# Edge counts with a row of degrees, and an own division of PSUM for the heads of the first attention

## The chip, the cores and the metric

The kernel runs on one core of a Trainium2 chip. The core has five engines with a program each: TensorE (PE in the profile; PEld is its weight load), VectorE (DVE), ScalarE (ACT), GpSimd (POOL) and SyncE (SP, which here issues DMAs). Each engine works through its instructions in their order and waits on semaphores for the others. The metric is the device time of one execution in microseconds (us): 1857.35 us is the median of three runs of the kernel before (1856.94 to 1857.70).

## The reference

The reference is a stack of four blocks on a graph of 625 nodes with 768 features and a list of edges (src, dst); each block is a graph layer and then an expert or feed-forward layer, each behind a layer norm and added to x. The change lies in the first graph layer alone, an attention of 12 heads with 64 features per head:

```
hv = h.reshape(n, H, DIN)                          # h = layernorm(x), H = 12
ft = einsum('nhd,od->nho', hv, W)
a1 = sum(ft * attn_l, -1);  a2 = sum(ft * attn_r, -1)
e = leaky_relu(a1[src] + a2[dst], 0.2)
m = segment_max(e, dst)
w = exp(e - m[dst])
alpha = w / maximum(segment_sum(w, dst)[dst], 1e-16)
agg = segment_sum(alpha[:, :, None] * ft[src], dst)
out = relu((agg + einsum('nhd,od->nho', hv, W_res)).reshape(n, H * DOUT))
x = x + out
```

Later layers (two graph convolutions among them) need the in-degree of each node: deg = segment_sum(1, dst), with a loop edge added, and its reciprocal root.

## The kernel before

All of it is one program, whose functions below issue instructions; a scheduler then decides the order in which they stand on each engine, and places the semaphores. Lines are those of the kernel before. Nodes are held as 5 tiles (t or s) of P = 125.

**Edge counts (L863 to L894).** The graph is turned into a dense matrix A[src, dst] of edge counts (AT, in f32, 125 x 5 x 625). The edges come as 85 chunks of 125. For each chunk DVE makes a one-hot matrix of the sources (ohs, L868, four rotating buffers) and one of the destinations (ohd, L863, where one column stands for two destinations: the second counts 4096), and PE multiplies them tile by tile (L875, five matmuls a chunk, 32 chunks accumulated in PSUM). Then ACT copies the sums out as integers (L883), DVE takes them apart (L885, L886) and adds them to AT (L892, L894). Between chunks PE also projects the features (L802, L810, L833).

**Before the heads.** ACT and DVE take the logarithm of the counts (L630, L631), and PE turns AT tile by tile for a mask (`mask_tile`, 25 transposes, L639), which ACT changes to 0 or a large number (L642).

**One head** is these steps, and the loop at L993 to L1026 issues them staggered over heads:

- `score` (L654 on ACT, L658 on POOL): weights of all pairs, from a row of a2 loaded by DMA and the logarithms.
- `gat_largest`: PE spreads a1 as a row over the partitions (L156, five transposes into a PSUM buffer, `spread_with`); DVE takes the largest over the neighbours (L666, one instruction per tile) and makes from it the offset u (L672, L673).
- `gat_exp`: PE spreads u as a row (L156 again, operand gat_u), DVE subtracts it (L686; one instruction for heads 0 to 9, five for heads 10 and 11), ACT takes the exponential (L688, five instructions).
- `gather`: PE multiplies the weights with the features (L138, ten matmuls of two passes each), ACT copies the result out (L943, gat_o).
- `back`: PE turns it (L958), DVE takes the reciprocal of the sum (L961) and adds each tile to res (L963). Every second head ACT clips the pair (L974) and POOL adds it to x (L1019); for the last pairs DVE does so (L1013, L982). DVE takes statistics of x for the next layer norm (L978).

**Degrees (L922 to L931).** For each tile of destinations five matmuls (L927) of AT with a column of ones, so 25 in all; ACT copies the five columns out (L931). They are called in the loop at i == 2.

**After the heads (L1026 to L1035).** POOL converts AT for later layers and adds the loops (L1028 to L1031), SP stores it (L1032), ACT and DVE make the reciprocal root of the degrees (L1033 to L1035). The last head's `back` also normalises x tile by tile and turns it for the next layer (L194 to L206, then L213 on PE and L217 on ACT). The next layer's first matmuls are L145.

**PSUM.** Every step above that writes PSUM takes its buffer from `ps()`: four rotating buffers of 128 x 1024 f32, two banks each, so the whole of PSUM. A step waits until the last reader of the buffer's user four turns before is done.

Of the kernel before, what the change touches and what calls it, by code (L numbers as in the profile page):

```python
# [19 lines left out]
N = 625  # L20
P = 125
# [18 lines left out]
class Net:  # L40
# [6 lines left out]
    def __init__(self, ctx, tc, a, out):  # L47
        self.tc, self.nc, self.a, self.out = tc, tc.nc, a, out
        self.turn = 0
        self.ctx = ctx  # L50
        nc = self.nc
        self.const = ctx.enter_context(tc.tile_pool(name="const", bufs=1))
        self.small = ctx.enter_context(tc.tile_pool(name="small", bufs=2))
        self.rows = ctx.enter_context(tc.tile_pool(name="rows", bufs=2))
        self.xnp = ctx.enter_context(tc.tile_pool(name="xnp", bufs=2))
        self.psum = ctx.enter_context(
            tc.tile_pool(name="psum", bufs=4, space=bass.MemoryType.PSUM)
        )
# [36 lines left out]
        self.iD = self.dram.tile([1, 2], U32, name="iD")  # L95
        self.counts = ExitStack()
        pool = self.counts.enter_context(tc.tile_pool(name="atr", bufs=1))
        self.ATr = pool.tile([128, NT, N + 1], F32R, name="ATr")
        self.which = pool.tile([2, 1], U32, name="which")
        self.many = pool.tile([P, NT], F32, name="many")  # L100
        self.open_counts()

    def open_counts(self):
        self.exact = ExitStack()
        self.AT = self.exact.enter_context(self.tc.tile_pool(name="at", bufs=1)).tile(
            [P, NT, N], F32, name="AT"
        )

    def ps(self):
        return self.psum.tile([128, 1024], F32, tag="ps", name="ps")  # L110

    @staticmethod
    def nv(t, rows, cols=P):
# [34 lines left out]

        return self.spread_with(col, rows)[0]

    def spread_with(self, col, rows):

        p = self.ps()
        pv = self.nv(p, rows)
        for t in range(NT):
            self.nc.tensor.transpose(  # L156
                pv[:, t, :], col(t).to_broadcast([P, rows]), self.ident[:P, :P]
            )
        return pv, p[:rows, NT * 128 : NT * 129]

    def row(self, name, cols, src=None):

# [467 lines left out]
        nc.scalar.activation(r, self.AT[:, s, :], AF.Ln, bias=self.tiny[:P], scale=2.0)  # L630
        nc.vector.scalar_tensor_tensor(r, r, BIG, r, ALU.mult, ALU.min)  # L631

    def mask_tile(self, mb, t, act=False):


        nc = self.nc
        pv = self.nv(self.ps(), P)
        for s in range(NT):
            nc.tensor.transpose(pv[:, s, :], self.AT[:, s, TILES[t]], self.ident[:P, :P])  # L639
        m = self.n3(mb[:, t, :])  # L640
        if act:
            nc.scalar.activation(m, pv, AF.Relu, bias=self.large[:P], scale=-BIG)  # L642
        else:
            nc.vector.tensor_scalar(m, pv, 0.5, BIG / 2, ALU.is_lt, ALU.mult)

    def gat_scores(self, w, a1, a2row, lc, a8=None):

# [12 lines left out]
    def gat_largest(self, pool, mb, a1, a2, row=None):  # L660

        nc = self.nc
        row, m = row or self.spread_with(lambda t: a1[:, t : t + 1], P)
        for t in range(NT):
            junk = pool.tile([P, N], F32, tag="junk", name="junk", bufs=1)
            nc.vector.tensor_tensor_reduce(  # L666
# [9 lines left out]
    def gat_exp(self, w, a1, u, a2=None, pieces=1):  # L676

        nc = self.nc
        if a2 is None:
            a2 = self.small.tile([P, NT], F32, tag="gat_2", name="gat_2")  # L680
            nc.scalar.activation(a2, a1, AF.Copy, scale=0.2)
        row = self.spread(lambda t: u[:, t : t + 1], P)
        w4 = w.rearrange("p t (k c) -> p t k c", c=P)
        for s in range(0, NT, NT // pieces):
            ws = w4[:, s : s + NT // pieces]
# [5 lines left out]
    def L0_gnn(self):  # L691
# [5 lines left out]
        with ExitStack() as ctx:  # L697
# [13 lines left out]
            with ExitStack() as c1:  # L711
# [141 lines left out]

                AT = self.AT
                G = 32
                for c0 in range(0, NC, G):
                    cs = range(c0, min(c0 + G, NC))
                    acc = [halves(self.ps()[:P])[:, :, 0:HN] for _ in range(3)]  # L860
                    for c in cs:
                        ohd = op.tile([P, HN + 1], BF16, tag="ohd", name="ohd")
                        nc.vector.tensor_scalar(  # L863
                            ohd, iota[:, 0 : HN + 1], key[:, c : c + 1], wt[:, c : c + 1],
                            ALU.is_equal, ALU.mult,
                        )
                        ohs = op.tile([P, NW], BF16, tag="ohs", name="ohs")
                        nc.vector.tensor_scalar(  # L868
                            ohs, iota, ef[:, 0, c : c + 1], None, ALU.is_equal
                        )  # L870
                        oh[0] = ohd
                        for piece in pieces.get(c, ()):
                            piece()
                        for j in range(NT):
                            nc.tensor.matmul(  # L875
                                acc[j // 2][:, j % 2, :], ohs[:, TILES[j]], ohd[:, 0:HN],
                                start=c == cs[0], stop=c == cs[-1],
                            )
                    first = c0 == 0
                    for j in range(3):  # L880
                        n = 2 if j < 2 else 1
                        raw = cp.tile([P, 2, HN], I32, tag="raw", name="raw", bufs=3)[:, 0:n]
                        nc.scalar.copy(raw, acc[j][:, 0:n])  # L883
                        hi = cp.tile([P, 2, HN], I32, tag="hi", name="hi")[:, 0:n]
                        nc.vector.tensor_scalar(hi, raw, 12, None, ALU.arith_shift_right)  # L885
                        nc.vector.tensor_scalar(raw, raw, 4095, None, ALU.bitwise_and)  # L886
                        at = AT[:, 2 * j : 2 * j + n]
# [9 lines left out]
            for s in range(NT):  # L897
                self.log_counts(lc, s)

            row = self.spread_with(lambda t: al[:, t, 0, 0:1], P)  # L900
            for t in range(NT):
                self.mask_tile(mb, t, act=True)
            self.prepare(router="L0_ffn_router")

            guard = big.tile([DH + 1, 1], F32, name="guard")
# [15 lines left out]

            def degrees():  # L922

                p = self.ps()[:P, 0:NT]
                for t in range(NT):
                    for s in range(NT):
                        nc.tensor.matmul(  # L927
                            p[:, t : t + 1], self.AT[:, s, TILES[t]], self.ones[:P, 0:1],
                            start=s == 0, stop=s == NT - 1,
                        )  # L930
                nc.scalar.copy(self.deg, p)  # L931

            def gather(h):

                w = ws[h]
                pv = self.nv(self.ps(), DH + 1)
                self.mm_nodes(
                    pv, [ft[:, s, h, :] for s in range(NT)],
                    [self.n3(w[:, s, :]) for s in range(NT)],
# [7 lines left out]
            def back(h, then=None):  # L947

                o = outs[h]
                p = self.ps()[:P, 0 : NT * 128].rearrange("p (t c) -> p t c", c=128)  # L950
                rden = self.small.tile([P, NT, 1], F32, tag="rden", name="rden")
                hs = slice(h * DH, (h + 1) * DH)
                for part in (range(4), range(4, NT)) if then else (range(NT),):
# [36 lines left out]
            for i in range(H + 4):  # L990
# [4 lines left out]
                if 0 <= i - 2 < H:  # L995
# [1 line left out]
                    self.gat_exp(  # L997
                        ws[h], a1[h], us[h], a1s[:, 0, :, h], pieces=1 if i < H else NT
                    )
                if i == 2:  # L1000
                    degrees()
                steps = [(back, i - 4), (gather, i - 3)]
                for f, h in steps if i < H else reversed(steps):
# [4 lines left out]
                if i == H + 1:  # L1008

                    for g in range(H // 2 - 1):  # L1010
# [11 lines left out]
                        for t in range(NT):  # L1022
                            stats(t, g)
            back(H - 1, then=last)

            for t in range(NT):  # L1026
                at, r = AT[:, t, :], self.ATr[:P, t, 0:N]
# [1575 lines left out]
```

## Time and profile before

| What | Value |
|---|---|
| median of three runs | 1857.35 us (1856.94 to 1857.70) |
| the profiled execution | 1859.18 us |
| its span, first to last instruction | 1857.5 us |
| mean granted clock of TensorE | 0.986 |
| busy share of the span, PE / DVE / POOL / ACT | 96% / 61% / 36% / 29% |
| chain that ended last: matmuls of L145 | 64% of the span |
| first counting matmul L875 in the chain | 24.89 us |
| start of the first L686 | 111.87 us |
| start of head 9's L686 | 196.67 us |
| first L145 of the next layer | 233.01 us |

The span is shorter than the execution's time by what lies around it (1.68 us). A line of the time line has the start, the duration, the engine, the line of the code, the operation, output and inputs with their shapes, and a count; in brackets stands how long the engine was idle before it and what ended that. PE's granted clock is a share of its full speed: 1.00 or, in some stretches, 0.50.

### The profile page before, as it was taken

What the parts mean: (1) busy time and instruction counts of PE and PEld (TensorE: products, weight loads), DVE (VectorE), ACT (ScalarE), POOL (GpSimd) and SP (SyncE); (2) the same over time, 40 slices, a digit from 0 to 9 for tenths busy, and PEclk for the clock granted to TensorE, in tenths of its full rate; (3) what the DMA queues carried; (4) which work ended last, traced back from release to release, by engine and by line L of the source; (5) the groups of instructions that cost most, each with busy time, mean ns of one, the idle gap of its engine ahead of it and who ended that gap; (6) DMA issues with size and microseconds to landing.
All of it is one profiled execution on the core that took longest, in us unless ns stands there. A gap on an engine that the chain in (4) does not pass through costs nothing.

```text
span 1857.5 us, 21937 instructions
## 1 busy us (share of the span) xinstructions
PE 1783.6 (96%) x8274; PEld 1275.4 (69%) x8274; DVE 1138.7 (61%) x2307; ACT 543.0 (29%) x979; POOL 667.1 (36%) x532
## 2 busy tenths in 40 slices
PE   8978899999999999999999999999999999999998
PEld 7854466557677766655776787878768888556765
DVE  8789866657666765575486655564756555154452
ACT  2468831114244433111211131231314323111200
POOL 0068666435410035753225322221335222401550
PEclk9969999999999999999999999999999999999999
DMA  2040143120300014514142211011012111020311
GB/s 55 24 146 35 57 116 115 55 85 23 97 26 27 1 53 144 159 41 136 42 136 94 85 43 60 26 60 35 6 40 68 54 56 39 0 102 26 110 59 33
DMA packets 71696, 119.29 MB, mean 64 GB/s; under 512 B 8609, under 2 KB 38531, under 8 KB 71591
## 3 DMA queue, kind: packets, MB, share of 16 engines
q1 hardware_dynamic: 71266, 117.80, 19.7%
q8 instruction: 65, 1.06, 0.2%
q14 instruction: 41, 0.33, 0.1%
q10 hardware_dynamic: 260, 0.09, 0.0%
q0 software_dynamic: 64, 0.01, 0.0%
HBM read 114.30 MB, written 3.58 MB: 63 GB/s over the span
## 4 chain that ended last, share of the span: by engine, by line
PE 80%; DVE 11%; ACT 4%; DMA 2%; issue 2%; POOL 0%; SPq 0%; DVEq 0%; ACTq 0%
PE ps L145 64%; PE ps L2081 2%; PE ps L1707 2%; PE ps L1739 2%; DVE av_junk L1541 2%; PE ps L875 2%; PE ps L138 2%; PE ps L1726 2%; DVE gat_w L686 1%; ACT gat_w L688 1%; PE ps L213 1%; PE ps L156 1%; DMA x<-in_x 1%; DMA av_w<-in_L_gnn_W 1%; PE ps L810 1%
## 5 line engine op out<-in xcount | busy, mean ns | idle before, releaser
L428 POOL TENSOR_TENSOR S<-w 128x384 f32<-128x384 f32 x40 | 41.9, 1052 | 390.8 <-PE ps L145 290.5
L145 PE MATMUL ps<-w,xT 128*125 128x384 f32 (+3 forms) x440 | 141.2, 474 | 0.0
L145 PE MATMUL ps<-xT,w 128*128 128x313 f32 x480 | 139.1, 430 | 0.7 <-ACT pr L1715 0.7
L145 PE MATMUL ps<-T,w 128*128 128x313 f32 x408 | 122.4, 430 | 8.9 <-DVE U L448 7.7
L658 POOL TENSOR_TENSOR gat_w<-gat_w,xT 125x625 f32<-125x625 f32 x60 | 86.2, 1472 | 118.4 <-DVE xT L631 96.3
L145 PEld LDWEIGHTS ps<-w,xT 128*125 128x125 f32 (+1 forms) x440 | 81.8, 188 | 52.5 <-issue 11.3
L145 PEld LDWEIGHTS ps<-xT,w 128*128 128x128 f32 x480 | 90.1, 191 | 33.9 <-ACT pr L1715 0.9
L145 PE MATMUL ps<-T,S 128*128 128x313 f32 x348 | 103.7, 431 | 1.7 <-DVE T L408 1.4
L145 PEld LDWEIGHTS ps<-T,w 128*128 128x128 f32 x408 | 75.4, 189 | 41.5 <-DVE U L448 10.1
L145 PE MATMUL ps<-xT,S 128*128 128x313 f32 x336 | 101.1, 430 | 0.0
L145 PE MATMUL ps<-w,S 128*125 128x384 f32 (+1 forms) x292 | 99.2, 486 | 0.0
L145 PE MATMUL ps<-w,hg 128*125 128x384 f32 x288 | 96.3, 486 | 0.0
L145 PE MATMUL ps<-hh,gat_w 125*125 125x257 f32 (+1 forms) x400 | 89.7, 379 | 0.0
L145 PE MATMUL ps<-w,x2T 128*125 128x384 f32 (+1 forms) x280 | 84.3, 450 | 0.9 <-DVE gat_u L673 0.9
L1541 DVE CUSTOM_DVE_ANT_0 av_junk<-av_w,av_a 128x512 bf16<-128x512 f32 (+1 forms) x80 | 81.5, 1018 | 3.7 <-DMA av_w<-in_L_gnn_W 1.8
L145 PEld LDWEIGHTS ps<-T,S 128*128 128x128 f32 x348 | 63.9, 189 | 28.7 <-ACT lt L456 4.4
L145 PEld LDWEIGHTS ps<-w,S 128*125 128x125 f32 (+1 forms) x292 | 54.8, 188 | 39.0 <-issue 0.7
L145 PEld LDWEIGHTS ps<-hh,gat_w 125*125 125x125 f32 x400 | 73.4, 187 | 11.0
L145 PEld LDWEIGHTS ps<-xT,S 128*128 128x128 f32 x336 | 62.0, 189 | 24.3 <-DVE lt L448 2.2
L145 PEld LDWEIGHTS ps<-w,hg 128*125 128x125 f32 x288 | 53.6, 188 | 36.5 <-issue 0.6
L138 PE MATMUL ps<-gat_w,ft 125*65 125x500 f32 (+1 forms) x240 | 69.8, 447 | 5.2 <-DVE gat_w L686 3.5
L875 PE MATMUL ps<-ohd,ohs 125*125 125x313 bf16 x425 | 64.0, 304 | 8.8 <-DVE ohs L868 8.8
(485 smaller groups left out, 3800.0 us busy)
## 6 DMA issues: line engine op xcount, KB each, us to landing
w<-in_L_ffn_phiT SPq DMA_DIRECT2D x8, 1536.0 KB
w<-in_L_gnn_W SPq DMA_DIRECT2D x8, 1536.0 KB
gate<-gD SPq DMA_DIRECT2D x24, 312.5 KB
w<-in_L_ffn_w SPq DMA_DIRECT2D x6, 1152.0 KB
w<-in_L_gnn_W SPq DMA_DIRECT2D x6, 1152.0 KB
av_w<-in_L_gnn_W SPq DMA_DIRECT2D x24, 256.0 KB
av_w<-in_L_gnn_W SPq DMA_DIRECT2D x16, 384.0 KB
w<-in_L_ffn_w SPq DMA_DIRECT2D x3, 1536.0 KB
```

The lines of the kernel that those rows point to most:

```text
L138: self.nc.tensor.matmul(pv[:, s, :], lhs[i], rhs[i][:, s, :], start=i == 0, stop=i == n - 1)
L145: self.nc.tensor.matmul(out, lhs[i], rhs[i], start=i == 0, stop=i == n - 1)
L156: self.nc.tensor.transpose(pv[:, t, :], col(t).to_broadcast([P, rows]), self.ident[:P, :P])
L213: nc.tensor.transpose(pv[:, k, :P], src[:, k * 128 : (k + 1) * 128], self.ident[:P, :P])
L428: nc.gpsimd.tensor_tensor(S1, A21, A22, ALU.add)
L658: nc.gpsimd.tensor_tensor(w[:, s, :], w[:, s, :], lc[:, s, :], ALU.add)
L875: nc.tensor.matmul(acc[j // 2][:, j % 2, :], ohs[:, TILES[j]], ohd[:, 0:HN], start=c == cs[0], stop=c == cs[-1],)
L1541: nc.vector.tensor_tensor_reduce(junk, wt, row, 1.0, 0.0, ALU.mult, ALU.add, dst)
L1707: nc.tensor.matmul(sv[r][:, s, :], qk[half[r], 0, TILES[t]], self.n3(qk[half[r], 1, :])[:, s, :], start=True, stop=True,)
L1726: nc.tensor.transpose(tv[:, s, :], pr[:, s * P : (s + 1) * P], self.ident[:P, :P])
L1739: nc.tensor.matmul(ov[half[r]], v[:, s, h * DH : (h + 1) * DH], pT[r][:, s, :], start=s == 0, stop=s == NT - 1,)
L2081: nc.tensor.matmul(pv[:, j, :], zTs[t][:, k, :], w2[k // 3][:, k % 3, js], start=k == 0, stop=False,)
```

## The change

The counting keeps four fixed one-hot buffers for the sources, two columns wider, and the extra columns are set to one once. The last of a chunk's five matmuls has 127 rows out in place of 125, so that row 126 of AT's last tile holds the number of edges of each destination. The degrees are then five matmuls (one per tile of destinations) that pick that row with a column of the identity matrix, and are called at i == 3. PSUM has a new division after the counting: one fixed buffer "gathered", one fixed buffer "turned", and two rotating ones; `gather` takes the first, `back` and the degrees the second, all rows the rotating ones. After the last `back` has been issued the division goes back to four rotating buffers. The masks' transposes are issued by source tile for three destination tiles at a time.

```
+    def open_psum(self, kept=()):
+        self.banks.close()
+        self.psum = self.banks.enter_context(
+            self.tc.tile_pool(name="psum", bufs=1, space=bass.MemoryType.PSUM)
+        )
+        self.kept = {k: self.psum.tile([128, 1024], F32, tag=k, name="ps") for k in kept}
+
+    def ps(self, kept=None):
+        if kept in self.kept:
+            return self.kept[kept]
+        return self.psum.tile(
+            [128, 1024], F32, tag="ps", name="ps", bufs=4 - len(self.kept)
+        )
...
-    def mask_tile(self, mb, t, act=False):
+    def mask_tile(self, mb, *ts, act=False):
...
-        pv = self.nv(self.ps(), P)
+        pvs = {t: self.nv(self.ps(("gathered", "turned", None)[t % 3]), P) for t in ts}
         for s in range(NT):
-            nc.tensor.transpose(pv[:, s, :], self.AT[:, s, TILES[t]], self.ident[:P, :P])
...
+            for t in ts:
+                nc.tensor.transpose(
+                    pvs[t][:, s, :], self.AT[:, s, TILES[t]], self.ident[:P, :P]
+                )
...
-        row = self.spread(lambda t: u[:, t : t + 1], P)
+        row = self.spread_with(lambda t: u[:, t : t + 1], P, "offsets")[0]
...
+                senders = [ep.tile([P, NW + 2], BF16, name=f"ohs{i}") for i in range(4)]
+                for ohs in senders:
+                    nc.gpsimd.memset(ohs[:, NW:], 1.0)
...
                         for j in range(NT):
+                            R = P if j < NT - 1 else P + 2
                             nc.tensor.matmul(
-                                acc[j // 2][:, j % 2, :], ohs[:, TILES[j]], ohd[:, 0:HN],
-                                start=c == cs[0], stop=c == cs[-1],
+                                acc[j // 2][:R, j % 2, :], ohs[:, j * P : j * P + R],
+                                ohd[:, 0:HN], start=c == cs[0], stop=c == cs[-1],
                             )
...
+            self.open_psum(("gathered", "turned"))
             row = self.spread_with(lambda t: al[:, t, 0, 0:1], P)
-            for t in range(NT):
-                self.mask_tile(mb, t, act=True)
+            for ts in ((0, 1, 2), (3,), (4,)):
+                self.mask_tile(mb, *ts, act=True)
...
             def degrees():
-                p = self.ps()[:P, 0:NT]
+                p = self.ps("turned")[:P, 0:NT]
                 for t in range(NT):
-                    for s in range(NT):
-                        nc.tensor.matmul(
-                            p[:, t : t + 1], self.AT[:, s, TILES[t]], self.ones[:P, 0:1],
-                            start=s == 0, stop=s == NT - 1,
-                        )
+                    nc.tensor.matmul(
+                        p[:, t : t + 1], self.ATd[: P + 2, NT - 1, TILES[t]],
+                        self.ident[: P + 2, P + 1 : P + 2], start=True, stop=True,
+                    )
...
-                pv = self.nv(self.ps(), DH + 1)
+                pv = self.nv(self.ps("gathered"), DH + 1)
...
-                p = self.ps()[:P, 0 : NT * 128].rearrange("p (t c) -> p t c", c=128)
+                p = self.ps("turned")[:P, 0 : NT * 128].rearrange("p (t c) -> p t c", c=128)
...
-                if i == 2:
+                if i == 3:
                     degrees()
...
             back(H - 1, then=last)
+            self.open_psum()
```

`ATd` is AT with all of its 128 partitions; "offsets" is not among the kept names, so u's row takes a rotating buffer. The second piece of the last head's `back` takes `ps()`, as before.

More of the change, by code (lines that the diff above doesn't have):

```diff
@@ L49, in __init__ @@
         self.turn = 0
+        self.banks = ctx.enter_context(ExitStack())
         self.ctx = ctx
@@ L55, in __init__ @@
         self.xnp = ctx.enter_context(tc.tile_pool(name="xnp", bufs=2))
-        self.psum = ctx.enter_context(
-            tc.tile_pool(name="psum", bufs=4, space=bass.MemoryType.PSUM)
-        )
+        self.open_psum()
         self.ident = self.const.tile([128, 128], F32, name="ident")
@@ L104, in open_counts @@
         self.exact = ExitStack()
-        self.AT = self.exact.enter_context(self.tc.tile_pool(name="at", bufs=1)).tile(
-            [P, NT, N], F32, name="AT"
-        )
-    def ps(self):
-        return self.psum.tile([128, 1024], F32, tag="ps", name="ps")
+        self.ATd = self.exact.enter_context(self.tc.tile_pool(name="at", bufs=1)).tile(
+            [128, NT, N], F32, name="AT"
+        )
+        self.AT = self.ATd[:P]
+    def open_psum(self, kept=()):
[10 more added lines that the diff above has]
+        )
     @staticmethod
@@ L149, in spread, with spread_with @@
         return self.spread_with(col, rows)[0]
-    def spread_with(self, col, rows):
-        p = self.ps()
+    def spread_with(self, col, rows, kept=None):
+        p = self.ps(kept)
         pv = self.nv(p, rows)
@@ L158, in spread_with @@
             )
-        return pv, p[:rows, NT * 128 : NT * 129]
+        return pv, p
     def row(self, name, cols, src=None):
@@ L631, in log_counts @@
         nc.vector.scalar_tensor_tensor(r, r, BIG, r, ALU.mult, ALU.min)
-    def mask_tile(self, mb, t, act=False):
+    def mask_tile(self, mb, *ts, act=False):
         nc = self.nc
-        pv = self.nv(self.ps(), P)
+        pvs = {t: self.nv(self.ps(("gathered", "turned", None)[t % 3]), P) for t in ts}
         for s in range(NT):
-            nc.tensor.transpose(pv[:, s, :], self.AT[:, s, TILES[t]], self.ident[:P, :P])
[L640 to L644, printed above, removed]
+            for t in ts:
+                nc.tensor.transpose(
+                    pvs[t][:, s, :], self.AT[:, s, TILES[t]], self.ident[:P, :P]
+                )
+        for t in ts:
+            m = self.n3(mb[:, t, :])
+            if act:
+                nc.scalar.activation(m, pvs[t], AF.Relu, bias=self.large[:P], scale=-BIG)
+            else:
+                nc.vector.tensor_scalar(m, pvs[t], 0.5, BIG / 2, ALU.is_lt, ALU.mult)
     def gat_scores(self, w, a1, a2row, lc, a8=None):
@@ L662, in gat_largest @@
         nc = self.nc
-        row, m = row or self.spread_with(lambda t: a1[:, t : t + 1], P)
+        row, p = row or self.spread_with(lambda t: a1[:, t : t + 1], P)
+        m = p[:P, NT * 128 : NT * 129]
         for t in range(NT):
@@ L852, in L0_gnn @@
                 pieces[70] = [to_rows]
-                AT = self.AT
+                AT = self.ATd
+                senders = [ep.tile([P, NW + 2], BF16, name=f"ohs{i}") for i in range(4)]
+                for ohs in senders:
+                    nc.gpsimd.memset(ohs[:, NW:], 1.0)
                 G = 32
@@ L859, in L0_gnn @@
                     cs = range(c0, min(c0 + G, NC))
-                    acc = [halves(self.ps()[:P])[:, :, 0:HN] for _ in range(3)]
+                    acc = [halves(self.ps())[:, :, 0:HN] for _ in range(3)]
                     for c in cs:
@@ L866, in L0_gnn @@
                         )
-                        ohs = op.tile([P, NW], BF16, tag="ohs", name="ohs")
+                        ohs = senders[c % 4]
                         nc.vector.tensor_scalar(
-                            ohs, iota, ef[:, 0, c : c + 1], None, ALU.is_equal
+                            ohs[:, 0:NW], iota, ef[:, 0, c : c + 1], None, ALU.is_equal
                         )
@@ L880, in L0_gnn @@
                     for j in range(3):
[L881 to L884, printed above, removed]
+                        n, R = (2, P) if j < 2 else (1, P + 2)
+                        raw = cp.tile([128, 2, HN], I32, tag="raw", name="raw", bufs=3)[:R, 0:n]
+                        nc.scalar.copy(raw, acc[j][:R, 0:n])
+                        hi = cp.tile([128, 2, HN], I32, tag="hi", name="hi")[:R, 0:n]
                         nc.vector.tensor_scalar(hi, raw, 12, None, ALU.arith_shift_right)
                         nc.vector.tensor_scalar(raw, raw, 4095, None, ALU.bitwise_and)
-                        at = AT[:, 2 * j : 2 * j + n]
+                        at = AT[:R, 2 * j : 2 * j + n]
                         for half, v in (
@@ L922, in degrees @@
             def degrees():
-                p = self.ps()[:P, 0:NT]
+                p = self.ps("turned")[:P, 0:NT]
                 for t in range(NT):
-                    for s in range(NT):
-                        nc.tensor.matmul(
-                            p[:, t : t + 1], self.AT[:, s, TILES[t]], self.ones[:P, 0:1],
-                            start=s == 0, stop=s == NT - 1,
-                        )
+                    nc.tensor.matmul(
+                        p[:, t : t + 1], self.ATd[: P + 2, NT - 1, TILES[t]],
+                        self.ident[: P + 2, P + 1 : P + 2], start=True, stop=True,
+                    )
                 nc.scalar.copy(self.deg, p)
@@ L1024, in L0_gnn @@
             back(H - 1, then=last)
+            self.open_psum()
             for t in range(NT):
-                at, r = AT[:, t, :], self.ATr[:P, t, 0:N]
+                at, r = self.AT[:, t, :], self.ATr[:P, t, 0:N]
                 nc.gpsimd.tensor_copy(r[: DH + 1, 0:1], outs[H - 3][:, 0:1])
```

## The prediction

> **What bounds the kernel now.** I read the engine table first (PE is busy for 96% of the span), then the chain of waits, then the time line and the windows of the first attention, since every edit lies there. The changed program's instructions stand in the same order on every engine from the first expert layer on, about 233 us into the span.
>
> From 233 us on, the chain is nearly all TensorE. Its three long transfers (av_w, at 831, 946 and 963 us, 14.3 us together) begin as the DVE step that frees their buffer, or the PE burst before them, ends. So a delay at 233 us is carried to the end one for one, and I only count when that point is reached. The first 233 us split into an opening, a steady loop over heads and a tail.
>
> The opening, time line of before (start, duration, engine, line, operation, operands, and in brackets the idle time before it and what ended it):
>
> ```profile
> 109.00 10.50 PE L927 MATMUL ps<-ones,AT 125*125 125x1 f32 x50
> ...
> 111.87 3.41 DVE L686 TENSOR_TENSOR gat_w<-gat_w,ps 125x3125 f32<-125x3125 f32 x1 [1.87 <-POOL gat_w L658]
> ...
> 122.33 3.41 DVE L686 TENSOR_TENSOR gat_w<-gat_w,ps 125x3125 f32<-125x3125 f32 x1 [2.55 <-PE ps L156]
> ...
> 134.51 8.05 PE L138 MATMUL ps<-gat_w,ft 125*65 125x500 f32 x20 [3.55 <-DVE gat_w L686]
> ...
> 143.14 0.81 DVE L666 CUSTOM_DVE_ANT_0 junk<-ps,mb 125x625 f32<-125x625 f32 x1 [2.78 <-PE ps L156]
> ```
>
> L686 runs once per head, so its starts are my clock: 111.87, 122.33, 131.00, 143.87 us for heads 0 to 3. The old degrees (L927) hold PE for 10.5 us, and head 1's row (L156) and L686 come after them.
>
> The steady loop, same view:
>
> ```profile
> 173.94 3.65 ACT L688 ACTIVATE gat_w<-gat_w,a1s 125x625 f32<-125x625 f32 x5 [0.26 <-DVE gat_w L686]
> ...
> 177.49 0.76 ACT L943 ACTIVATE gat_o<-ps,guard 65x625 f32<-65x625 f32 x1
> ...
> 178.30 0.81 PE L156 MATMUL ps<-ident,gat_u 125*125 125x125 f32 x5 [1.61 <-ACT gat_o L943]
> ...
> 179.22 3.41 DVE L686 TENSOR_TENSOR gat_w<-gat_w,ps 125x3125 f32<-125x3125 f32 x1 [0.33 <-PE ps L156]
> ```
>
> Four hops close a ring of 8.73 us: exponentials L688, copy out L943 (which frees a PSUM buffer), the row of u (L156), the subtraction L686. The windows of one such period (stretch; length, then busy PE, PEld, DVE, ACT, POOL; granted clock) show who is next:
>
> ```profile
> 170.49:179.22 8.73, 7.12 (x37) 4.10 (x37) 8.39 (x20) 8.47 (x13) 8.47 (x7) 1.00 0.11 36
> ```
>
> DVE at 8.39, ACT at 8.47: removing a wait can win 0.3 us per head at most. L686 of head 9 starts at 196.67. The tail:
>
> ```profile
> 211.41 0.76 ACT L943 ACTIVATE gat_o<-ps,guard 65x625 f32<-65x625 f32 x1
> ...
> 214.16 1.55 POOL L1019 TENSOR_TENSOR x<-x,res 125x640 f32<-125x640 f32 x1
> ...
> 226.99 4.17 PE L213 MATMUL ps<-ident,xn 125*128 125x125 f32 x18 [3.44 <-DVE lt_r L198]
> ...
> 233.01 10.79 PE L145 MATMUL ps<-xT,w 128*128 128x313 f32 x36
> ```
>
> From L686 of head 9 (call it T) the first turn L213 comes at T+30.3 and the first L145 at T+36.3.
>
> **Edits at nothing.** Four memsets (125x2) for the ones: POOL's 128x5 memset takes 0.11 us, 0.44 in all, at 3 us, before the first one-hot at 5.16; uncovered they cost 0.44. The counting matmul with 127 rows out keeps its 313 columns; the copies of that chunk are as wide as before. Mask turning by source tile: the 25 transposes already stand so on PE in the program before, so that edit moves nothing. The five transfers L1032 follow L1031 on SP and come up to 1.55 earlier; nothing here waits for them. Head 0's first row moves behind the counting, where PE waits from 89.8 to 95.4; without that cover 0.7 us. The new degrees are 5 matmuls, 10 passes of 0.21 (10.50/50) = 2.1 us, and stand before the wait for u of head 0.
>
> **Opening: gain 5.7.** DVE does the same 26 maxima (L666) before L686 of head 3 in both programs, plus one reciprocal (0.2) after. Its three waits above, 1.87 + 2.55 + 2.78 = 7.20, are what can go: the first is filled by five more L666 (L686 of head 0 slides to about 114.4), the second was L927, the third followed from it. What is late next is the short wait on each row, 0.33 as in steady heads, times four: 7.20 − 0.2 − 1.3 = 5.7, so head 3 at 138.2. Upper end 7.0 (no such waits). Lower end 3.4: a first gather at half clock takes 8.05, not the 5.75 of the row at 122.02, and PE's queue behind it loses 2.3.
>
> **Steady loop: loss 2.4.** All gathers now share one PSUM buffer. In every second head (5, 7, 9) the changed order has the first matmul of the next gather (L138, two passes, spacing 0.42, so 0.85) ahead of the u row on PE, and it waits for L943 of the gather before. What queues behind it is the u row, and L686 waits for that. That link: L688 3.65 + L943 0.76 + L138 0.85 + L156 0.81 + L686 3.42 + handoffs 0.16 = 9.65. The other head's link lies on ACT: L688 3.64 + L943 0.66 + L974 0.63 + L654 3.63 = 8.56. A pair takes 18.21 against 17.46, three pairs 54.6, plus 0.6 for one stretch at half clock (the window from 152.63 to 161.76 stands at clock 0.81 and its period at 9.13): 55.2, against 196.67 − 143.87 = 52.8. Ends: DVE the only bound, about 8.5 a head, 51.2 (−1.6); both heads of a pair with the queued matmul, 57.9 (+5.1). Head 9 then starts at 193.4, 3.3 ahead.
>
> **Tail: loss 6.9.** (1) The last x += res on POOL (L1019) moves behind all conversions L1028 to L1031, which take 7.7 us after L943 of head 9 (212.23 to 221.47, less L1019's own 1.55). That copy ends at T+15.8 (15.5 before), so L1019 ends at T+15.8+7.7+1.55 = T+25.05. (2) DVE has 5 statistics of that piece (1.05) ahead of the outputs of heads 9 and 10: L961 with 5 L963 (1.25), L1013 1.57, statistics 1.05, L961 with 5 L963 1.25: T+31.2. Only then is the single "turned" buffer free for the last head: L958 0.7, and 3.2 from its L961 to L213 as in before (223.80 to 226.99): T+35.1, against T+30.3. (3) With two rotating buffers in place of four, the turns wait for copies out: the last head's fifth transpose waits for L217 of the second turn, the fourth turn for L963 of that transpose, the first L145 for L217 of the fourth turn: 8.1 from first turn to L145 (4.9 to the fifth transpose, 0.9 to its L963, 1.5 turn, 0.8 copy), against 6.02. Sum: T+43.2 against T+36.3. Ends: +2.4 if POOL and DVE don't decide (PE and ACT alone: the last gather started at T+20.0, and now waits for head 10's copy, T+15.8 + 5.43 + 0.76 + handoffs = T+22.4, with L145 as far behind it as before); +9.7 if both late gathers run at half clock (2 x 2.6) ahead of it.
>
> **First burst: loss 1.4.** The granted clock is 0.5 from 225.06 to 235.3, so 36 passes of L145 take 10.79 with 2.3 us at half. At full clock that is 9.64. PE is sparser before it now; one and a half steps of 3.41 at half (the length in steps of which this trace's stretches at half clock come) would make 12.2. Ends: 0 and +2.3.
>
> **Sum**: −5.7 + 2.4 + 6.9 + 1.4 = +5.0 us. The profiled execution took 1859.18 (span 1857.5, 1.68 around it), so this becomes 1864.2; it is 1.83 above the median of 1857.35, and on the median's scale I forecast 1862.3.
>
> **Weighed against a rule.** The steady windows with 1.6 us idle at one place per head show clock 1.00, so I leave the loop at full clock. The Trainium skill, "TensorE: Matmul & The Clock Gate", section "A second HAM failure mode: psum-queue depth-cycling", speaks against this change more strongly: a PE that idles a little at each turn of PSUM buffers swings between half and full clock. By that rule each of the 8 gathers from head 4 on could take 8.05 in place of 5.43, up to 2.6 us more on one head in two, and the sum would be about +15; no run here shows such a loop.
>
> **Rivals.** (A) Slower, as summed; own range 1861 to 1868. (B) No change: POOL's queue doesn't decide the tail. For it: L1019 has no PE or ACT behind it, only statistics. Tail then +2.4, burst 0 to 1.4: −5.7 + 2.4 + 2.4 + 1 = about 0, 1857.5. Against: the statistics stand ahead of L961 in an in-order queue. (C) Faster: the heads become bound by DVE. For it: 8.39 busy of 8.73, and u no longer needs the buffer that L943 frees in even heads. It decides if the queued L138 finds L943 done, that is if a pair takes under 17.2: −5.7 − 1.6 + 2.4 = −4.9, 1852.4. Against: the 1.61 wait on L943 in the row above is the same wait. (D) The degrees don't leave the path: without the 5.7, 1868. Against: 2.1 us in a stretch where PE waits.
>
> **Numbers.** A 0.50, B 0.30, C 0.17, D 0.03. A measurement of this kernel can tell about 0.2%, 3.7 us, from no change. Faster 0.17, same 0.30, slower 0.53. The extreme ends of all terms add up to −6.2 and +13.7, which would need every one at once. The range 1853 to 1867 leaves out most of C and the end of A and D, about 0.2.
>
> **What would show it.** L686 of head 3 near 138 and no PE block at 109 to 119 confirm the opening; pairs of L686 18.2 apart, with L138 x2 ahead of L156, the loop; L1019 behind L1031 and L961 waiting for it, the tail; L145 starting near 237 and its burst over 12 us, the rest. A first L145 before 232 would make the forecast wrong.

## The result and the profile after

The changed kernel takes 1860.31 us (median of 14 runs, 1858.10 to 1863.06), the kernel before 1857.12 us in the 14 runs beside them (1853.14 to 1858.18). The ratio is 1.0022, with a 95% interval of 1.0013 to 1.0030: slower by 2.4 to 5.6 us, 4.1 by the ratio. The forecast was +5.0, with 1853 to 1867 as its range. The profiled execution of the changed kernel took 1859.69 us, its span is 1858.0.

The lines of the changed kernel are shifted. What was L927 is now L947, L686 is L702, L688 is L704, L138 is L149, L943 is L963, L156 is L167, L1019 is L1039, L978 is L998, L958 is L978, L961 is L981, L213 is L224, L217 is L228 and L145 is L156. Of those that stand in brackets only, L658 is now L673, L974 is L994, L963 is L983 and L198 is L209. In the experiments some lines stand one or two off these.

One thing must be taken out before the two time lines are laid beside each other. The counting ends 1.76 us later in this profile (the last group of copies out of sums, L903, starts at 93.87; L883 of before at 92.11). The experiments below put most of this down to scatter, so I measure each stretch from its own start.

The opening, time line of the changed kernel:

```profile
106.58 2.26 PE L947 MATMUL ps<-ident,AT 127*125 127x1 f32 x10
...
116.27 3.43 DVE L702 TENSOR_TENSOR gat_w<-gat_w,ps 125x3125 f32<-125x3125 f32 x1
...
124.04 3.45 DVE L702 TENSOR_TENSOR gat_w<-gat_w,ps 125x3125 f32<-125x3125 f32 x1
...
131.22 3.41 DVE L702 TENSOR_TENSOR gat_w<-gat_w,ps 125x3125 f32<-125x3125 f32 x1
...
139.63 3.41 DVE L702 TENSOR_TENSOR gat_w<-gat_w,ps 125x3125 f32<-125x3125 f32 x1 [0.26 <-POOL gat_w L673]
```

The block of 10.5 us is 2.26 now, and three of the four subtractions stand without a wait. Head 3 comes 139.63 − 93.87 = 45.76 us after the end of the counting, against 143.87 − 92.11 = 51.76: a gain of 6.0.

The loop, same view, one pair of heads:

```profile
148.02 3.41 DVE L702 TENSOR_TENSOR gat_w<-gat_w,ps 125x3125 f32<-125x3125 f32 x1
...
155.02 0.77 ACT L963 ACTIVATE gat_o<-ps,guard 65x625 f32<-65x625 f32 x1
...
155.84 1.05 PE L149 MATMUL ps<-gat_w,ft 125*65 125x500 f32 x2 [1.61 <-ACT gat_o L963]
...
156.73 0.71 PE L167 MATMUL ps<-ident,gat_u 125*125 125x125 f32 x5
...
157.54 3.41 DVE L702 TENSOR_TENSOR gat_w<-gat_w,ps 125x3125 f32<-125x3125 f32 x1 [0.21 <-PE ps L167]
```

The old wait of 1.61 us on the copy out is still there, and it is now the gather's first matmul that waits, with the row of u behind it. The windows of the three pairs (stretch; length, then busy PE, PEld, DVE, ACT, POOL; granted clock, DMA share, GB/s):

```profile
139.63:157.54 17.91, 15.38 (x75) 8.84 (x76) 17.70 (x41) 17.91 (x26) 16.31 (x12) 1.00 0.10 36
157.54:175.63 18.09, 16.12 (x72) 8.99 (x72) 16.96 (x40) 16.33 (x24) 15.48 (x12) 0.91 0.09 35
175.63:193.51 17.88, 14.44 (x72) 8.28 (x72) 16.86 (x40) 16.21 (x24) 15.43 (x12) 1.00 0.10 36
```

The three pairs take 53.88 against 52.80, a loss of 1.1: a pair is 17.96 on average, against 17.60 in before (17.46 in before's two pairs at full clock). Within a pair the subtractions aren't evenly apart: 8.39 and 9.52 us in the first, 7.52 and 10.57, and 7.52 and 10.36 in the others. The tail, time line again:

```profile
216.30 1.53 POOL L1039 TENSOR_TENSOR x<-x,res 125x640 f32<-125x640 f32 x1
...
217.87 1.07 DVE L998 BATCH_NORM_STATS2 st<-x 125x6 f32<-125x128 f32 x5 [5.49 <-POOL x L1039]
...
221.01 1.06 DVE L998 BATCH_NORM_STATS2 st<-x 125x6 f32<-125x128 f32 x5
...
222.41 0.66 PE L978 MATMUL ps<-ident,gat_o 65*125 65x65 f32 x5
...
223.11 0.20 DVE L981 RECIPROCAL rden<-ps 125x5 f32<-125x5 f32 x1 [1.03 <-PE ps L978]
...
224.53 0.62 PE L978 MATMUL ps<-ident,gat_o 65*125 65x65 f32 x4 [1.46 <-DVE res L983]
...
228.38 2.92 PE L224 MATMUL ps<-ident,xn 125*128 125x125 f32 x12 [3.23 <-DVE lt_r L209]
...
236.63 11.72 PE L156 MATMUL ps<-xT,w 128*128 128x313 f32 x36 [0.88 <-ACT xT L228]
```

From head 9's subtraction at 193.51 the first turn comes at +34.9 and the first matmul of the next layer at +43.1, against +30.3 and +36.3: a loss of 6.8. That burst is 11.72 long, against 10.79: 0.9 more. POOL's sum does stand late, and five statistics wait 5.49 us for it, as forecast. But the statistics are done at 222.07, and the next reciprocal waits 1.03 more for PE: which of the two decides had to be tried.

### The profile page after: what moved, and what is told of

Read it like the earlier page. It is cut to its first block, busy times and chain, and to the rows that moved or that the text cites. A ratio compares the mean times of both kernels' runs of the same rounds, so it can differ in the third digit from the quotient of the medians.

```text
span 1858.0 us, 21855 instructions
## 1 busy us (share of the span) xinstructions
PE 1778.9 (96%) x8234; PEld 1269.8 (68%) x8234; DVE 1139.6 (61%) x2307; ACT 542.7 (29%) x979; POOL 666.6 (36%) x536
## 4 chain that ended last, share of the span: by engine, by line
PE 79%; DVE 11%; ACT 6%; DMA 3%; issue 1%; POOL 0%; SPq 0%; ACTq 0%; DVEq 0%
PE ps L156 63%; PE ps L2102 2%; PE ps L1728 2%; PE ps L1760 2%; ACT gat_w L704 2%; PE ps L895 2%; DVE av_junk L1562 2%; PE ps L1747 2%; ACT gat_w L669 1%; PE ps L149 1%; PE ps L224 1%; DMA x<-in_x 1%; DVE gat_w L702 1%; DVE junk L682 1%; PE ps L826 1%
## 5 line engine op out<-in xcount | busy, mean ns | idle before, releaser
L156 PE MATMUL ps<-xT,w 128*128 128x313 f32 x480 | 140.0, 432 | 1.6 <-ACT xT L228 0.9
L156 PE MATMUL ps<-w,xT 128*125 128x384 f32 (+3 forms) x440 | 141.2, 474 | 0.0
L156 PE MATMUL ps<-T,w 128*128 128x313 f32 x408 | 122.3, 430 | 8.1 <-DVE U L459 7.5
L673 POOL TENSOR_TENSOR gat_w<-gat_w,xT 125x625 f32<-125x625 f32 x60 | 86.0, 1472 | 110.2 <-DVE xT L642 97.9
L156 PEld LDWEIGHTS ps<-w,xT 128*125 128x125 f32 (+1 forms) x440 | 81.8, 188 | 52.5 <-issue 11.3
L156 PEld LDWEIGHTS ps<-xT,w 128*128 128x128 f32 x480 | 90.4, 192 | 35.5 <-issue 1.3
L156 PE MATMUL ps<-T,S 128*128 128x313 f32 x348 | 103.7, 431 | 2.0 <-DVE T L419 1.4
L156 PEld LDWEIGHTS ps<-T,w 128*128 128x128 f32 x408 | 75.4, 189 | 40.2 <-DVE U L459 9.8
L156 PE MATMUL ps<-xT,S 128*128 128x313 f32 x336 | 101.1, 430 | 0.0
L156 PE MATMUL ps<-w,S 128*125 128x384 f32 (+1 forms) x292 | 99.2, 486 | 0.0
L156 PE MATMUL ps<-w,hg 128*125 128x384 f32 x288 | 96.3, 486 | 0.0
L156 PE MATMUL ps<-hh,gat_w 125*125 125x257 f32 (+1 forms) x400 | 89.7, 379 | 0.0
L156 PE MATMUL ps<-w,x2T 128*125 128x384 f32 (+1 forms) x280 | 84.3, 450 | 0.9 <-DVE gat_u L689 0.9
L156 PEld LDWEIGHTS ps<-T,S 128*128 128x128 f32 x348 | 63.9, 189 | 29.0 <-ACT lt L467 4.6
L156 PEld LDWEIGHTS ps<-w,S 128*125 128x125 f32 (+1 forms) x292 | 54.7, 188 | 39.0 <-issue 0.7
L156 PEld LDWEIGHTS ps<-hh,gat_w 125*125 125x125 f32 x400 | 73.4, 187 | 11.0
L156 PEld LDWEIGHTS ps<-xT,S 128*128 128x128 f32 x336 | 62.0, 189 | 24.3 <-DVE lt L459 2.1
L156 PEld LDWEIGHTS ps<-w,hg 128*125 128x125 f32 x288 | 53.6, 188 | 36.6 <-issue 0.6
L895 PE MATMUL ps<-ohd,ohs 125*125 125x313 bf16 (+1 forms) x425 | 66.7, 313 | 11.5 <-DVE ohs L887 11.5
L149 PE MATMUL ps<-gat_w,ft 125*65 125x500 f32 (+1 forms) x240 | 70.4, 447 | 6.3 <-ACT gat_o L963 6.3
```

Of the source, the lines that this page charges most:

```text
L149: self.nc.tensor.matmul(pv[:, s, :], lhs[i], rhs[i][:, s, :], start=i == 0, stop=i == n - 1)
L156: self.nc.tensor.matmul(out, lhs[i], rhs[i], start=i == 0, stop=i == n - 1)
L673: nc.gpsimd.tensor_tensor(w[:, s, :], w[:, s, :], lc[:, s, :], ALU.add)
L895: nc.tensor.matmul(acc[j // 2][:R, j % 2, :], ohs[:, j * P : j * P + R], ohd[:, 0:HN], start=c == cs[0], stop=c == cs[-1],)
```

## The experiments

**Theory.** The degrees as a row win about 6 us in the opening; the single buffers and the two rotating ones lose it in the tail, a little in the loop. **Rivals.** The counting with 127 rows out costs 1.8; POOL's queue, not PSUM, makes the tail; the opening's gain isn't the degrees' at all.

**The row of counts alone** (the rest is the changed kernel):

```
-            self.open_psum(("gathered", "turned"))
...
             back(H - 1, then=last)
-            self.open_psum()
```

> The row of counts and the five-matmul degrees of the change, with the four rotating PSUM buffers of before through all heads; masks issued by source tile. Theory (the degrees gain about 6 us in the opening, and the loss lies in the division of PSUM behind it): head 3's subtraction starts about 6 us earlier than in before as far as the old ring of buffers lets it, no loss in the loop (8.73 a head) and in the tail, so 1851 to 1856. Rival 1 (the counting with 127 rows out costs the 1.8 us by which the changed kernel's counting ended later in its profiled run): the counting ends 1.8 later here too. Rival 2 (the gain in the opening needs the own buffers, since in a ring of four the row of u waits for a gather's copy): head 3 within 2 us of before, and the time within 2 us of 1857.

Measured: 1856.12 us, ratio 1.000 (0.9991 to 1.0008). Loop and tail are those of before (36.1 from head 9 to L145). Rival 2 holds: the degrees alone win nothing. Head 1 is 122.33 − 92.11 = 30.2 us behind the counting in before and 27.5 here, but head 3 is 52.1 behind it, against 51.76. The counting ends at 93.19, 1.1 later than in before, with rival 1 saying 1.8; the other runs speak on this below. The time line of this run shows where the gain is given back:

```profile
131.36 3.41 DVE L702 TENSOR_TENSOR gat_w<-gat_w,ps 125x3125 f32<-125x3125 f32 x1 [2.72 <-PE ps L167]
...
134.83 8.19 PE L149 MATMUL ps<-gat_w,ft 125*65 125x500 f32 x20 [3.04 <-DVE gat_w L702]
...
143.05 0.78 ACT L962 ACTIVATE gat_o<-ps,guard 65x625 f32<-65x625 f32 x1 [4.60 <-PE ps L149]
```

In the ring of four, head 1's gather waits 3.04 us until the subtraction has read the row in its buffer, then takes 8.19 at a low clock, and the next rows queue behind it. In the changed kernel, with the own buffer, head 1's gather starts at 132.49, 1.27 us into that subtraction and without waiting for its end, and takes 5.42.

**The division alone**, with the old degrees at their old place and the counting of the change:

```
-                    nc.tensor.matmul(
-                        p[:, t : t + 1], self.ATd[: P + 2, NT - 1, TILES[t]],
-                        self.ident[: P + 2, P + 1 : P + 2], start=True, stop=True,
-                    )
+                    for s in range(NT):
+                        nc.tensor.matmul(
+                            p[:, t : t + 1], self.AT[:, s, TILES[t]], self.ones[:P, 0:1],
+                            start=s == 0, stop=s == NT - 1,
+                        )
...
-                if i == 3:
+                if i == 2:
```

> The division of PSUM and the masks by source tile, with the counting of before's width kept as in the change and the old degrees of 25 matmuls, called at i == 2. Theory: the loss in loop and tail of the changed kernel (1.1 + 6.8 + 0.9 by its profile) stays and the opening's gain shrinks by what the 8 more us of degrees on PE cost, so 3 to 5 us above the changed kernel, 1863 to 1866. Rival (the degrees were hidden, the opening's gain comes from the order of DVE alone): the same time as the changed kernel, 1860.

Measured: 1866.54 us, ratio 1.0053 (1.0038 to 1.0067), 6.2 more than the changed kernel and a little above the theory's range. The time line of this run, with the old degrees and head 3's subtraction:

```profile
106.96 10.66 PE L948 MATMUL ps<-ones,AT 125*125 125x1 f32 x50
...
144.85 3.41 DVE L702 TENSOR_TENSOR gat_w<-gat_w,ps 125x3125 f32<-125x3125 f32 x1 [0.26 <-POOL gat_w L673]
```

So with the own buffers in place the degrees are worth 6 us of time; head 0's subtraction is at 121.49, where the changed kernel has 116.27. The tail is the changed kernel's to 0.1 us (43.1). Head 3 is 144.85 − 94.26 = 50.6 us behind the counting, 1.2 sooner than in the kernel before and 4.8 later than in the changed kernel. So at head 3 the degrees alone win nothing (0.3 lost), the buffers alone win 1.2, and together they win 6.0.

**Four rotating buffers again from head 9's gather on**, ahead of the last three gathers and the last four backs:

```
             for i in range(H + 4):
+                if i == H:
+                    self.open_psum()
...
             back(H - 1, then=last)
-            self.open_psum()
```

> The changed kernel, but PSUM goes back to four rotating buffers as the loop comes to i == 12, ahead of the last three gathers and backs and of the turns. Theory (the tail's 6.8 us come from the single buffers for gathers and backs, which chain gather, copy out and back of the last three heads, and from only two buffers for the turns): head 9 starts as in the changed kernel, the first L145 about 36 to 38 us after it in place of 43, so 5 to 7 us less than the changed kernel, 1853 to 1855, below both. Rival (POOL's sum L1019 behind the conversions decides the tail): L1019 stays there, the first L145 at 40 us or more after head 9, and at most 3 us less than the changed kernel, 1857 to 1860.

Measured: 1852.07 us, ratio 0.9977 (0.9968 to 0.9986): 8.2 less than the changed kernel, and faster than before. L145 comes 38.4 after head 9 and its burst takes 9.65, so 4.7 of the tail's loss of 6.8 and all of the burst's are gone. But the rival's condition, that POOL's sum stays where it is, does not hold here. The sum (L1041 in this run) has moved ahead of most conversions, 18.3 us after head 9 in place of 22.8:

```profile
212.51 1.54 POOL L1041 TENSOR_TENSOR x<-x,res 125x640 f32<-125x640 f32 x1
```

It has moved so in every run below with more than two rotating buffers in the tail. So this run alone does not part the division from POOL's queue; the run with later conversions does.

**Only backs have an own buffer**, three rotating ones for the rest:

```
-            self.open_psum(("gathered", "turned"))
+            self.open_psum(("turned",))
```

> The changed kernel with one own buffer only, for backs and degrees; gathers and rows share three rotating ones. Theory (a single buffer for gathers costs the loop 0.2 to 0.4 a head and chains the last gathers): the period of the heads is again 8.73, and the tail is shorter than 43 us by the wait of each late gather for the copy before it, 1 to 3 us; so 1855 to 1858. Rival (the single buffer for backs, and the two for the turns, make the tail): the same tail within 1 us and 1859 to 1861.

Measured: 1860.21 us, ratio 1.0019 (1.0010 to 1.0028). The loop is back at 8.73 (151.99 to 160.72, 169.85 to 178.58), as the theory has it, and L145 is at 38.6 after head 9, sooner than its 40 to 42. The total is not the theory's and falls in the rival's range for another reason: head 3 comes 50.5 after the counting, not 45.8, so the opening's gain is mostly gone, and the burst takes 12.4. The time line of this run:

```profile
124.75 8.43 PE L149 MATMUL ps<-gat_w,ft 125*65 125x500 f32 x20 [3.67 <-DVE gat_w L702]
```

Here it is head 0's gather that shares a ring with the rows and waits 3.67 us for the subtraction, as head 1's did with four rotating buffers. The own buffer for backs is not enough for the opening; whether the one for gathers is enough by itself was not run.

**POOL's conversions later**, anchored at head 10's copy out, so that L1039 isn't behind them:

```
-                nc.gpsimd.tensor_copy(r[: DH + 1, 0:1], outs[H - 3][:, 0:1])
+                nc.gpsimd.tensor_copy(r[: DH + 1, 0:1], outs[H - 2][:, 0:1])
```

> The changed kernel, with the conversions on POOL anchored at head 10's copy out in place of head 9's, so that they no longer stand ahead of the sum L1019 (L1039 in the changed kernel's lines). Theory 1 (the single buffers chain the last gathers on PE, and POOL's queue is only level with them: in the changed kernel's profile the statistics behind the sum end at 222.07, and DVE then waits 1.03 more for PE's turn of head 10): the first turn L213 still 34 to 35 us after head 9's subtraction, the time within 2 us of the changed kernel's 1860. Theory 2 (POOL's queue decides the tail, as the prediction had it): first turn 3 us or more earlier, 1856 to 1857.

Measured: 1859.94 us, ratio 1.0016 (1.0007 to 1.0025), the changed kernel's time. The time line of this run:

```profile
211.75 1.54 POOL L1039 TENSOR_TENSOR x<-x,res 125x640 f32<-125x640 f32 x1 [4.53 <-ACT res L994]
...
216.83 1.07 DVE L998 BATCH_NORM_STATS2 st<-x 125x6 f32<-125x128 f32 x5
...
219.41 0.66 PE L978 MATMUL ps<-ident,gat_o 65*125 65x65 f32 x5
...
220.11 0.20 DVE L981 RECIPROCAL rden<-ps 125x5 f32<-125x5 f32 x1 [2.21 <-PE ps L978]
```

Head 9 is at 191.72 here. From there the sum is at +20.0 in place of +22.8 and the last statistics at +25.1 in place of +27.5, and DVE only waits longer (2.21 in place of 1.03) for PE's turn of head 10. The first turn comes at +33.7 and the first L145 at +41.9, both 1.2 earlier. So POOL's queue was worth about 1 us of the tail, and PE's chain the rest.

**Which buffers the tail needs**: from i == 12 on, one own buffer only, in two kernels.

```
             for i in range(H + 4):
+                if i == H:
+                    self.open_psum(("gathered",))
```

> The changed kernel, but from i == 12 on only the own buffer for gathers is kept, and backs, rows and turns share three rotating ones. Theory 1 (the single buffer for gathers chains the last three heads, the other two things cost the rest): first turn 33 to 35 us after head 9's subtraction, as in the changed kernel (34.9), first L145 6 us behind it in place of 8.2, so 1857 to 1859. Rival (the single buffer for backs is what costs): first turn at 32 or 33, like the run with four buffers (32.4), 1853 to 1855.

```
             for i in range(H + 4):
+                if i == H:
+                    self.open_psum(("turned",))
```

> The changed kernel, but from i == 12 on only the own buffer for backs is kept, and gathers, rows and turns share three rotating ones. Theory 1 (gathers' single buffer chains the last heads): with it gone, first turn 32 to 33 us after head 9's subtraction, first L145 6 to 7 behind it, 1854 to 1857. Rival (the single buffer for backs costs): first turn 34 to 35 as in the changed kernel, 1857 to 1859. The two kernels must add up to what the return to four buffers won (8 us) if the two costs don't hide each other.

Measured: 1855.25 us (0.9997, 0.9987 to 1.0006) with the gathers' own buffer kept, 1856.84 (1.0006, 0.9997 to 1.0016) with the backs'. First turn at 33.1 and 33.5 after head 9, first L145 at 39.8 and 40.9, bursts 11.4 and 12.3. The time lines, first the last head's gather with the gathers' buffer kept, then the last head's back with the backs' buffer kept:

```profile
214.91 5.47 PE L149 MATMUL ps<-gat_w,ft 125*65 125x500 f32 x20 [1.17 <-ACT gat_o L963]
```

```profile
221.32 0.62 PE L978 MATMUL ps<-ident,gat_o 65*125 65x65 f32 x4 [1.46 <-DVE res L983]
```

Each wait is that of the buffer kept: in the first kernel the last back waits 0.33 only, in the second the last gather does not wait. Giving up the backs' buffer wins 5.1, giving up the gathers' 3.5, both 8.2: the two costs nearly add up, though POOL's sum, worth about 1, has moved in both kernels and is counted twice. The first kernel's first turn is where the theory had it, its time nearer to the rival's; the second's time is the theory's, its first turn between the two. Neither story is enough alone. By the medians the backs' buffer costs more than the gathers' (each goes with the lack of a third rotating one), but the two intervals just overlap.

**The division for the first heads only**, four rotating buffers from i == 7 on:

```
             for i in range(H + 4):
+                if i == 7:
+                    self.open_psum()
...
             back(H - 1, then=last)
-            self.open_psum()
```

> The changed kernel, but PSUM goes back to four rotating buffers as the loop comes to i == 7, so the own buffers serve the opening and the first heads only. Theory (the opening's 6 us are worth having, the loop's pairs of 18 in place of 17.46 and the tail aren't): heads 6 to 9 again 8.73 apart, tail as in before (36.3 from head 9 to the first L145), so first L145 near 228 to 230 after a counting that ends as in before; 1850 to 1852, as fast as the return at i == 12 or up to 2 us faster. Rival (the loop's loss comes from half clock in the gathers and not from the shared buffer): heads still 9 us apart, 1852 to 1854.

Measured: 1849.73 us, ratio 0.9963 (0.9950 to 0.9977), 6.9 us faster than before by the ratio. Its median is below the run with the return at i == 12, but the two intervals overlap, so that it is the faster of the two is not shown. The time line of this run:

```profile
195.00 3.41 DVE L702 TENSOR_TENSOR gat_w<-gat_w,ps 125x3125 f32<-125x3125 f32 x1 [0.21 <-PE ps L167]
...
225.31 4.17 PE L224 MATMUL ps<-ident,xn 125*128 125x125 f32 x18 [3.44 <-DVE lt_r L209]
...
230.84 9.65 PE L156 MATMUL ps<-xT,w 128*128 128x313 f32 x36
```

Head 9 to first turn is 30.3, as in before. Heads 6 to 9 are not all 8.73 apart (10.16, 8.73, 9.12), since two gathers ran partly at half clock here (7.74 and 6.97 us in place of 5.43); this much of the rival holds.

## Why the prediction was right

The direction was right and the size near (+5.0 forecast, +4.1 by the ratio, +3.2 between the medians), and three of four terms were close. Their sum was less so: in the profiles the four add up to −6.0 + 1.1 + 6.8 + 0.9 = +2.8. That the first L145 came at 236.63, just where the forecast put it (233.01 − 5.7 + 2.4 + 6.9 = 236.6), is luck: 1.76 of these 3.6 us is the late counting.

- *Opening*: forecast −5.7, measured −6.0. Head 0 comes 22.4 us after the counting, as worked out (114.4 − 92.1 = 22.3). But the prediction gave the whole gain to the degrees. The runs with one half of the change each show that it belongs to the pair: at head 3 the degrees win nothing without the own buffers and 4.8 with them, and the own buffers alone win 1.2. That a gather in the ring of four waits for a row's buffer, then runs at a low clock and delays head 3 was not in the prediction's sum for the degrees.
- *Loop*: forecast +2.4, measured +1.1. The mechanism is the one named (the first matmul of the next gather ahead of the row of u). The pair was mis-sized, 18.21 in place of 17.91 and 17.88 in the two at full clock, and half clock cost 0.2 in the third (18.09), not 0.6. The pair is also split otherwise than by the two links of 9.65 and 8.56: the first subtraction comes 7.5 to 8.4 after the one before it, the second 9.5 to 10.6.
- *Tail*: forecast +6.9, measured +6.8, with the first turn at +34.9 (forecast +35.1) and L145 at +43.1 (forecast +43.2). The step that put POOL's sum and the statistics behind it on the path was wrong: moved out of the way, they move the first turn by 1.2 of the 4.6 that it came later, and change the time by less than the runs can tell. PE's own chain, which the prediction priced as the lower end at T+32.7, was slower than priced: the last gather starts at T+23.6 in place of T+22.4, since head 10's gather took 7.17 at a low clock in place of 5.43, and the last back waits 1.46 us until DVE has read head 10's turn out of the one "turned" buffer. So the total came out nearly exact partly by luck. From first turn to L145 the two rotating buffers cost what was forecast (8.25, forecast 8.1), and with four again it is 5.9.
- *Burst*: forecast +1.4, measured +0.9.
- *Carried to the end one for one*: not quite in this pair of profiles. By the starts of DVE's same steps, the changed kernel is 4.6 behind at 255 us, 3.9 at 350, 2.3 from 384 on, and 1.0 from 975 to the end. Of this, 1.6 lie between 350 and 384 us, where before's granted clock was 0.94 (340 to 370 us) and the changed kernel's 1.00; and 1.3 at the transfers of av_w at 946 and 963 us, where every other profiled kernel gains 0.5 to 1.3 on that one profile of before too. Why 0.7 went by 350 us stays open.
- *The late counting* (1.8 us) is for the most part not the change's: with the same counting, the profiles of the other kernels have its end between 92.3 and 94.3, two of them at 92.3, against 92.11 in the one profile of before. A kernel with the 127 rows alone was not run, and nothing here rules out a cost of 0.1 to 0.2.

Of the rivals, the one of a faster kernel (heads bound by DVE) fell: it needed pairs under 17.2 us, and they took 17.9 to 18.1. In two of three DVE is busy for 16.9 or 17.0, with the wait on the copy out still in them; in the first DVE is at 17.70, but ACT never idles (17.91 of 17.91). The one of no change was near the truth in its statement (POOL's queue doesn't decide the tail; it is worth about 1 us) but not its consequence, since PE's chain costs nearly as much. Of the clock rule weighed in the prediction (the Trainium skill, "TensorE: Matmul & The Clock Gate", section "A second HAM failure mode: psum-queue depth-cycling"), the trace shows a little: pairs at clock 1.00, 0.91 and 1.00, two gathers stretched from 5.43 to 6.74 and 7.17, and the other gathers from head 1 on at full clock.

## What to carry to other kernels

A division of PSUM is a choice per stage: here the own buffers were worth 6 us while the pipeline filled, together with the shorter degrees, and cost 0.4 us per pair in the steady loop and 8 us where the last heads drain (about 1 of them by way of POOL's queue), so give it back as soon as the stage that needs it is over. A freed engine and a freed buffer can be worth little apart and much together, so try a two-part change in both halves before crediting either. And where two chains meet within a microsecond, name both as the bound: moving the one that you see last moves the end by the difference only.

## What the runs showed that I had not expected

The length of the first burst of the next layer (36 passes of L145) goes by the clock that it meets, not by anything in it: 9.65 to 9.73 us in the three experiments with four buffers in the tail (clock 1.00 from 236 us on), 10.79 in before, and 11.4 to 12.4 in all six kernels with an own buffer there (clock 0.50 from 232 to 240 us in the changed kernel). In the changed kernel it starts at 236.63 and the clock over 236 to 246 us is 0.77, so at half for some 4 us of the burst, which makes 9.65 + 2 = 11.7. So a tail that leaves the clock at half is paid twice, the second time with up to 2.7 us in work that nobody touched. What in the tail decides how long the clock stays at half was not tested: before has four buffers there too, and still meets 2.3 us of it.

In the counting too, the clock stands at 0.76 between 24 and 31 us in some profiles (the changed kernel's, the division alone, the division for the first heads) and at 1.00 in others with the same instructions. The counting ends at 93.9 to 94.3 us in these three, and at 92.3 to 93.2 in the others, so 0.7 to 2 us sooner. A single profile can't tell a change of that size.
